# A selective scan on one core: input of state 0 made on GpSimd, end states copied on GpSimd, state sums evicted by a strand of their own, operation costs of the planner revised

## The chip, the cores and the metric

The kernel runs on one core of a Trainium2 chip. The metric is device time in microseconds (us). A run of the kernel before takes 10310.45 us, the median of three (10307.8 to 10314.3).

The engines are named as in the profile: PE is TensorE's matmul queue and PEld its weight loads, DVE is VectorE, ACT is ScalarE, POOL is GpSimd, and SP is SyncE, which here only issues DMAs. Other than SP's, no DMA queue carries the transfers of the kernel's loops.

## The reference

Four layers follow each other on an input of 8 samples x 256 channels x 32 x 32: an attention block with a convolutional feed-forward, a second attention with an MLP, a quantised bottleneck, and a Mamba layer (the fourth). The change lies in the Mamba layer, and in the cost table that orders the other three too. The Mamba layer, cut to what matters:

```python
def step(h, inp):
    u_t, dt_t, B_t, C_t = inp
    dA = jnp.exp(dt_t[:, :, None] * A)
    h = h * dA + dt_t[:, :, None] * B_t[:, None, :] * u_t[:, :, None]
    y = jnp.einsum('bdn,bn->bd', h, C_t)
    return (h, y)

x = silu(causal_conv4(x) + conv_b)               # x, z = split(u @ W_in.T)
x_dbl = x @ W_x.T                                # 16 for dt, 16 for B, 16 for C
dt = softplus(x_dbl[..., :16] @ W_dt.T + b_dt)
y = (selective_scan(x, dt, -exp(A_log), B, C) + x * D) * silu(z)
out = y @ W_out.T
```

There are 512 inner channels d and 16 states n for each. It runs over the 1024 pixels in four directions (row-wise, column-wise, and both backwards), and the four results are added. For one state n, four arrays over (channel, pixel) matter: the decay `dA`, the scan's input `dt * u * B`, the scan's result `h`, and `h * C`, which is summed over n.

## The kernel before

**Two phases.** `phase_a` does the first three layers and writes 8-bit-valued codes to DRAM. `phase_b` does the Mamba layer. In the profile phase_b begins at about 3745 us.

**Order.** The order of all instructions is fixed when the program is built. Each job is a generator (a "strand") that yields operations or conditions. `_Order.run` picks, again and again, the operation whose planned start is earliest; ties go to the lower rank. Planned starts come from `_Op.cost`, a formula for each engine and kind of operation, from `LATENCY` between engines (0.35 us), and from records of when each 512-element piece of a tile was written or read (`_Op.blocks`). The planned times decide only the order in each engine's queue. On the chip the engines wait on semaphores, in that order. Where an engine is planned to be free at the same time for several ready operations, the rank alone decides. `phase_a` uses the same planner; where PE is planned to have a gap, its `fill` puts in small bf16 matmuls.

**Blocks and groups.** A *block* n is one half (512 pixels) of one direction of one sample: 8 samples x 4 directions x 2 halves = 64 blocks. A *group* g is one state s of one block: 1024 groups. In a group the 512 channels are four tiles c of 128 partitions, worked in pairs p. `place[0]` is the group that the scans have reached.

**One group**, by strand:

- `scales` (ACT): four `dbu` tiles. The product dt*u lies transposed in `duT`, with pixels on partitions, so that B of state s is one value for each partition and ACT can multiply by it as its scale operand.
- `turns` (PE): sixteen 128x128 transposes bring `dbu` back to channels on partitions, into PSUM tiles `db` (three banks).
- `decays` (ACT): four `da` tiles, exp(dt * A), with five buffers.
- `scans` (DVE): four scans over 512 pixels, from `da` in SBUF and `db` in PSUM, into a pair tile `h` (six pairs). In a direction's second half they start from `st`, the end states of the first half.
- `ends` (ACT, only in the first half of a direction): copies the last column of each pair to `st`, two values per partition.
- `products` (POOL): each pair times the row C of state s, which `rows` (SP) loads, broadcast to 128 partitions, into `cb` (three buffers). The product is made in place. It comes only after `ends` has dealt with the pair, since `ends` reads what the product overwrites.
- `sums` (PE): transposes the product and adds it into four PSUM banks `py` over all 16 states. After the last state of three blocks in four the banks are moved to `yT`, by ACT and DVE, inside the same strand.

**Around it.** `ahead` starts the preparation of later blocks when the scans reach a given group. `mixed` makes the convolutions (`xs`) and `x_dbl` of block n+2. `steps` makes dt of block n+1, then (POOL) `tmp` = dt * xs, and its transposes into `duT`. `tables` runs silu and softplus on ACT, which takes three table loads. `outputs` makes the gate and the last product of the sample before.

The lines that the prediction's steps touch are: `_Op.__init__` (the costs), the rooms at the head of `phase_b`, `xdbl` in `mixed`, `dt` in `steps`, and the strands `scales`, `turns`, `rows`, `scans`, `ends`, `products`, `sums` and `ahead`. All instructions that the planner emits carry the one line L136 in the profile, so groups are told apart by their tiles.

Of the kernel before, what the change touches and what calls it, by code (L numbers as in the profile page):

```python
# [20 lines left out]
F32 = mybir.dt.float32  # L21
U8 = mybir.dt.uint8
BF16 = mybir.dt.bfloat16
# [6 lines left out]
P = 128  # L30
# [11 lines left out]
DC = DI // P  # L42
TH = HALF // P
PAD = 3
RND = 12582912.0
# [54 lines left out]
class _Op:  # L100


    def __init__(self, engine, method, args, kw):
        self.engine, self.method, self.args, self.kw = engine, method, args, kw
        out, ins = args[0], [a for a in (*args[1:], *kw.values()) if isinstance(a, bass.AP)]
        self.reads = {k for a in ins for k in self.blocks(a)}
        self.writes = {k for a in (out, kw.get("accum_out")) if a is not None for k in self.blocks(a)}
        self.landing = 0.0
        n = max(math.prod(a.shape[1:]) for a in (out, *ins)) / 1024
        near = all(a.space == out.space and out.space != PSUM for a in ins)  # L110
        if engine == "tensor":
            x = kw.get("rhs", ins[0])
            n = math.prod(x.shape[1:]) / 1024
            move = method == "transpose" or kw.get("is_transpose", False)
            self.cost = max(0.06, (0.22 if x.shape[0] < 20 else 0) + n * (0.93 if move else 0.44 if x.dtype != F32 else 1.76 if n > 0.2 else 2.1))
        elif engine == "vector":
            fast = near and method in ("tensor_scalar", "tensor_copy")
            both = near and method == "tensor_tensor"
            scan = method == "tensor_tensor_scan"
            self.cost = 0.04 + n * (2.2 if scan else 0.57 if fast else 1.1) + (0.3 if fast or both else 0)  # L120
        elif engine == "scalar":
            self.cost = 0.05 + 0.87 * n + (0.13 if len(ins) > 1 else 0)
        elif engine == "gpsimd":
            self.cost = 0.17 + 2.17 * n if method == "tensor_tensor" else 0.3 + n
        else:
            self.cost, self.landing = 0.1, 3.0

    @staticmethod
    def blocks(a):
        step = max(1, a.ap[0][0])  # L130
        lo = a.offset % step
        hi = lo + sum((n - 1) * abs(s) for s, n in list(a.ap)[1:])
        return [(a.name, k) for k in range(lo // 512, hi // 512 + 1)]

# [38 lines left out]
class _Order:  # L173
# [62 lines left out]
    def run(self):  # L236
        while self.strands:
# [16 lines left out]
            for o in ops:  # L254
                o.emit(self.nc)
                for k in o.reads:
                    self.read.setdefault(k[0], {})[k] = (t + cost, e)
                for k in o.writes:
                    self.written.setdefault(k[0], {})[k] = (t + cost + o.landing, e)
# [882 lines left out]
def phase_b(ctx, tc, i, col, ident, codes, w_parts, out):  # L1142
# [14 lines left out]
    xi_room = _Room(rooms, "xi", DC, [P, N + 2 * PAD])  # L1157
    xs_room = _Room(rooms, "xs", 11, [P, HALF])
    dt_room = _Room(rooms, "dt", 2 * DC, [P, HALF])
    du_room = _Room(rooms, "du", 2, [P, TH, DI])  # L1160
    db_room = _Room(rooms, "dbu", 12, [P, DI])
    da_room = _Room(rooms, "da", 5, [P, HALF])
    h_room = _Room(rooms, "h", 6, [P, 2, HALF])
    cb_room = _Room(rooms, "cb", 3, [P, HALF])
    tmp_room = _Room(rooms, "tmp", 2, [P, HALF])
    z_room = _Room(rooms, "z", DC, [P, HALF])
# [40 lines left out]
    def hs(h):  # L1207
        return slice(h * HALF, (h + 1) * HALF)
# [58 lines left out]
    def mixed(n):  # L1267
# [24 lines left out]
        def xdbl():  # L1292
# [6 lines left out]
            if d.c_d is None:  # L1299
                d.c_d = dr.tile([DS, N], F32, name="c_d", tag="c_d")  # L1300
                d.bT = sp.tile([P, NT, DS], F32, name="bT", tag="bT")
            yield S.dma_start(d.c_d[:, hs(h)], xd[DS : 2 * DS])
            done.add("xd")
# [11 lines left out]
    def steps(n):  # L1315
# [6 lines left out]
        def dt(c):  # L1322
# [11 lines left out]
            raw[n][c] = o  # L1334
            yield lambda: "soft" in done
            d.dt[c, h] = o
            t = yield from take(tmp_room)
            yield G.tensor_tensor(t, o, d.xs[c, h], ALU.mult)
            yield lambda: h in d.duT
            room, pt = yield from lend()  # L1340
            yield [T.transpose(pt[:, k * P : (k + 1) * P], t[:, k * P : (k + 1) * P], ident) for k in range(TH)]
            put(tmp_room, t)
            yield V.tensor_copy(d.duT[h][:, :, c * P : (c + 1) * P], pt.rearrange("p (t k) -> p t k", t=TH))
            put(room, pt)
            done.add(("du", c))

        return [dt(c) for c in range(DC)]


    dirs = [_Dir(b, bool(swap), back) for b in range(B) for swap in range(2) for back in (False, True)]  # L1350
    blocks = [(d, h) for d in dirs for h in d.halves]
    xis = {(b, swap): {} for b in range(B) for swap in (False, True)}
    raw = {n: {} for n in range(len(blocks))}
    gates = {(b, h): {} for b in range(B) for h in range(2)}

# [91 lines left out]


    groups = [(n, d, h, s) for n, (d, h) in enumerate(blocks) for s in range(DS)]
    dbu, db, da, hh, cbs = {}, {}, {}, {}, {}  # L1450
    place = [0]

    def scales():

        for g, (n, d, h, s) in enumerate(groups):
            yield lambda: {("du", c) for c in range(DC)} | {"bT"} <= d.done[h]
            for t in range(TH):
                src, b = d.duT[h][:, t], d.bT[:, h * TH + t, s : s + 1]
                o = yield from take(db_room)
                yield A.activation(o, src, AF.Identity, scale=b)  # L1460
                dbu[g, t] = o

    def turns():
        for g, (n, d, h, s) in enumerate(groups):
            for c in range(DC):
                yield lambda: all((g, t) in dbu for t in range(TH))
# [26 lines left out]
    def rows():  # L1493
        for g, (n, d, h, s) in enumerate(groups):
            yield lambda: "xd" in d.done[h]
            o = yield from take(cb_room)
            yield S.dma_start(o, d.c_d[s, hs(h)].partition_broadcast(P))
            cbs[g] = o

    def scans():  # L1500
        for g, (n, d, h, s) in enumerate(groups):
            step, first = -1 if d.back else 1, h == d.halves[0]
            place[0] = g
            if d.st is None:
                d.st = sp.tile([P, DC * DS], F32, name="st", tag="st")
            for c in range(DC):
                if c % 2 == 0:
# [4 lines left out]
                    x[:, ::step], da[g, c][:, ::step], db[g, c][:, ::step],  # L1512
                    0.0 if first else d.st[:, a : a + 1], ALU.mult, ALU.add,
                )
                put(da_room, da.pop((g, c)))
                put(ps_room, db.pop((g, c)))
                if c % 2:
                    hh[g, c // 2] = pair

    kept, scaled = {}, {}  # L1520

    def ends():

        for g, (n, d, h, s) in enumerate(groups):
            for p in range(2):
                yield lambda: (g, p) in hh
                pair, c = hh.pop((g, p)), 2 * p
                if h == d.halves[0]:
                    e = 0 if d.back else HALF - 1
                    o = d.st.rearrange("p (c s) -> p c s", s=DS)[:, c : c + 2, s : s + 1]  # L1530
                    yield A.copy(o, pair[:, :, e : e + 1])
                kept[g, p] = pair

    def products():
        for g, (n, d, h, s) in enumerate(groups):
            for p in range(2):
                yield lambda: (g, p) in kept and g in cbs
                pair = kept.pop((g, p))
                yield G.tensor_tensor(pair, pair, cbs[g].unsqueeze(1).to_broadcast([P, 2, HALF]), ALU.mult)
                scaled[g, p] = pair  # L1540
            put(cb_room, cbs.pop(g))

    def sums():

        for g, (n, d, h, s) in enumerate(groups):
# [27 lines left out]
            if s == DS - 1 and n % 4 != 1:  # L1573
                if n % 4 != 3:
                    yield lambda: clear[h]
                    clear[h] = False
                for t in range(TH):
                    o = yT[:, h * TH + t, :]
                    if n % 4 == 3:
                        yield V.tensor_tensor(o, py[t], o, ALU.add)  # L1580
                    elif t % 2:
                        yield V.tensor_copy(o, py[t])
                    else:
                        yield A.copy(o, py[t])
                    put(py_room, py[t])
                if g == len(groups) - 1:
                    spare.append(py_room)
                if n % 4 > 1:
                    for j in fold(d.b, d.swap, h):
                        order.add((0, n), j)  # L1590

    def ahead():

        for n in range(len(blocks)):
# [6 lines left out]
            if k is not None:  # L1601
                jobs += zip((1, 2, 3, 5, 9), mixed(k))
            if m is not None:
                jobs.append((6, tables(k, m, z)))
            if n % 4 == 1 and n + 3 < len(blocks):
# [28 lines left out]
    for rank, f in enumerate((scans, turns, products, sums, decays, scales, rows, ahead)):  # L1634
        order.add((1, rank), f())
    order.add((0, -2), ends())
    order.run()
# [118 lines left out]
```

## Time and profile before

| what | value |
|---|---|
| median of 3 runs | 10310.45 us (10307.8 to 10314.3) |
| the profiled execution, whole | 10303.42 us |
| its span, first to last instruction | 10301.6 us |
| around the span | 1.8 us |
| stretch 0 to 3600 us (phase_a): PE / DVE / ACT / POOL busy | 3386.04 / 2188.84 / 2597.26 / 897.55 us |
| first and last copy of `bT` on DVE's 63 from bank `pp` (blocks 1 to 63) | 3766.4 and 10057.7 us |
| so one block of phase_b | 6291.3 / 62 = 101.5 us |
| mean granted TensorE clock | 0.940 |

How it is read: the busy time of an engine is the union of its instructions. The records of two instructions that follow directly overlap a little on ACT and DVE: one `da` or `dbu` activation shows 710 to 714 ns, but in an unbroken row they start 0.61 to 0.62 us apart. So for loads per block the busy share is used, and for one instruction more or less the spacing. Matmul ends are modelled. Idle time is put down to the engine that the profile takes for the releaser.

### The profile page before, as it was taken

Reading aid. Unit: us, or ns where it says so; the run is one execution under the profiler, and the core shown is the slowest. Engines: PE = TensorE matmul, PEld = TensorE weight load, DVE = VectorE, ACT = ScalarE, POOL = GpSimd, SP = SyncE. Lnnn points to the kernel's source line nnn. Section 1 sums busy time; section 2 is a strip of 40 time slices with the busy share of each in tenths; the row PEclk is TensorE's granted clock in tenths of the full one; section 3 lists DMA queues with packets and bytes.
Section 4 is the critical chain, followed back from the end, with each engine's and each line's share of the span. In section 5 each row is a group of like instructions: output and inputs, shape, how many; then the busy total and the mean of one; then the engine's idle time right before and its main releaser. Section 6 shows DMA issues by size and latency. Waiting matters only on the chain.

```text
span 10301.6 us, 149772 instructions
## 1 busy us (share of the span) xinstructions
PE 9415.7 (91%) x55378; PEld 5953.1 (58%) x55499; DVE 7759.3 (75%) x8675; ACT 8514.4 (83%) x15869; POOL 6131.8 (60%) x2988
## 2 busy tenths in 40 slices
PE   9989989999999989989898999899989999989988
PEld 3333323333333347777776777777777777777676
DVE  6367467575667458888887888888888888888788
ACT  7867677867666759988898998989898889899888
POOL 1433032242121048878787787778787778787778
PEclk7988989989888899999999999999999999999999
DMA  2000000000000011112111112111111111111111
GB/s 58 30 19 17 21 21 19 17 26 17 13 17 9 17 34 51 53 44 59 46 52 53 46 52 59 43 52 56 49 51 48 56 50 49 55 52 46 57 43 52
DMA packets 219616, 415.83 MB, mean 40 GB/s; under 512 B 25137, under 2 KB 67505, under 8 KB 213762
## 3 DMA queue, kind: packets, MB, share of 16 engines
q1 hardware_dynamic: 218882, 406.24, 13.1%
q8 instruction: 437, 7.16, 0.3%
q14 instruction: 297, 2.43, 0.1%
HBM read 358.43 MB, written 37.22 MB: 38 GB/s over the span
## 4 chain that ended last, share of the span: by engine, by line
PE 28%; ACT 22%; DVE 8%; issue 3%; POOL 1%; DMA 1%; DVEq 0%; SPq 0%; POOLq 0%; ACTq 0%
PE pp L136 11%; PE py L136 9%; ACT da L136 9%; PE db L136 8%; ACT dbu L136 8%; DVE h L136 7%; ACT L136 2%; ACT xs L136 1%; ACT dt L136 1%; POOL h L136 1%; ACT L145 1%; DMA wi<-w_in 1%; DVE ys L136 1%; ACT st L136 0%; ACT z L136 0%
## 5 line engine op out<-in xcount | busy, mean ns | idle before, releaser
L136 POOL TENSOR_TENSOR h<-h,cb 128x1024 f32<-128x1024 f32 x2048 | 4813.3, 2373 | 1039.1 <-DVE h L136 367.0
L136 ACT ACTIVATE da<-dt,am 128x512 f32<-128x512 f32 x4096 | 2872.0, 714 | 543.2 <-DVE h L136 537.6
L136 ACT ACTIVATE dbu<-du,bT 128x512 f32<-128x512 f32 x4096 | 2798.1, 710 | 15.4 <-PE db L136 13.6
L136 PE MATMUL db<-ident,dbu 128*128 128x128 f32 x16384 | 2385.7, 280 | 362.2 <-DVE h L136 322.6
L136 DVE TENSOR_TENSOR_SCAN h<-da,db 128x512 f32<-128x512 f32 x2048 | 2338.9, 1202 | 460.2 <-ACT da L136 131.9
L136 DVE TENSOR_TENSOR_SCAN h<-da,st,db 128x512 f32<-128x512 f32 x2048 | 2465.9, 1262 | 258.8 <-ACT da L136 139.3
L136 PEld LDWEIGHTS db<-ident,dbu 128*128 128x128 f32 x16384 | 1885.2, 143 | 875.4 <-DVE h L136 539.6
L136 PE MATMUL py<-ident,h 128*128 128x128 f32 x16384 | 2141.8, 278 | 92.4 <-POOL h L136 75.5
L136 PEld LDWEIGHTS py<-ident,h 128*128 128x128 f32 x16384 | 1878.3, 143 | 227.0 <-POOL h L136 144.2
L136 DVE TENSOR_REDUCE stats<-bank 128x1 f32<-128x512 f32 x1536 | 983.4, 684 | 545.1 <-PE bank L136 544.0
L136 ACT ACTIVATE bank<-bank,stats 128x512 f32<-128x512 f32 x1536 | 1024.9, 672 | 432.1 <-DVE stats L136 424.5
L136 PE MATMUL bank<-big,big 32*128 32x512 f32 x4096 | 987.3, 713 | 37.9 <-ACT bank L136 27.7
L136 POOL TENSOR_TENSOR mid<-mid,mid 128x961 f32<-128x961 f32 (+2 forms) x192 | 397.2, 2076 | 992.9 <-ACT mid L136 663.6
L136 ACT ACTIVATE exps<-bank 128x512 f32<-128x512 f32 x1536 | 796.5, 620 | 165.9 <-PE bank L136 156.6
L136 PE MATMUL pp<-xi,cvd 128*128 128x512 f32 x1488 | 687.8, 598 | 1.6 <-DVE ys L136 1.6
L136 PEld LDWEIGHTS bank<-big,big 32*128 32x128 f32 x4096 | 334.7, 204 | 523.7 <-issue 219.7
L136 DVE SCALAR_TENSOR_TENSOR mid<-mid,cols,mid 128x961 f32<-128x961 f32 (+1 forms) x384 | 601.6, 1567 | 6.3
L136 PE MATMUL bank<-exps,big 128*32 128x512 f32 (+1 forms) x3072 | 547.9, 621 | 3.7 <-ACT exps L136 3.7
L136 PE MATMUL bank<-big 32*128 32x512 f32 x2048 | 517.4, 724 | 32.1 <-ACT bank L136 21.5
L136 POOL TENSOR_TENSOR tmp<-dt,xs 128x512 f32<-128x512 f32 x256 | 320.9, 1273 | 322.0 <-ACT dt L136 224.4
L136 POOL TENSOR_SCALAR big<-big,ga,gs 128x512 f32<-128x512 f32 x64 | 67.7, 1070 | 712.3 <-DVE gs L136 385.5
L136 POOL TENSOR_TENSOR big<-big,mid 128x961 f32<-128x961 f32 (+1 forms) x128 | 315.2, 2472 | 270.7 <-ACT mid L136 268.6
(204 smaller groups left out, 9116.4 us busy)
## 6 DMA issues: line engine op xcount, KB each, us to landing
cb<-c_d SPq DMA_DIRECT2D x1024, 256.0 KB, 3.3
wi<-w_in SPq DMA_DIRECT2D x192, 192.0 KB, 3.5
big<-in_x_dram SPq DMA_DIRECT2D x16, 1024.0 KB, 5.0
kept<-big SPq DMA_DIRECT2D x16, 1024.0 KB, 4.5
big<-kept SPq DMA_DIRECT2D x16, 1024.0 KB, 4.8
xf<-codes SPq DMA_DIRECT2D x48, 256.0 KB, 3.8
big<-big SPq DMA_DIRECT2D x16, 512.0 KB, 6.5
codes<-low SPq DMA_DIRECT2D x32, 256.0 KB, 2.0
```

The source lines that it names most:

```text
L136: return getattr(getattr(nc, self.engine), self.method)(*self.args, **self.kw)
L145: nc.scalar.preload_act_table_set("natural_log_exp_and_others")
```

## The change

**State 0 takes another way** (`OWN = 1`). For s = 0 `scales` and `turns` do nothing. A new strand `direct` loads the row B of state 0, broadcast to 128 partitions, and lets POOL multiply `tmp` (dt * xs, with channels on partitions) by it in place. The scans of s = 0 read this SBUF tile in place of a PSUM bank. For that, `tmp` becomes two pair tiles that are kept until these scans are done; the copy of B and C in DRAM (`c_d`) has 32 rows and not 16; and one row buffer `br` is added. `dbu` goes from 12 to 10 buffers.

**End states.** `ends` is gone. `products` copies the end states on POOL ahead of each product. `st` is four small tiles, each with two buffers.

**Eviction.** Moving `py` to `yT` becomes a strand of its own, `moved`, at rank (0, -3), the first of all.

**Times of the preparation.** The convolutions of block n+2 start at groups 0, 1, 2, 3 (1, 2, 3, 5 before), `x_dbl` at 8 (9), the tables at 4 (6). The four `tmp` products no longer follow the softplus at once: they wait for groups 5, 7, 9 and 11.

**The planner.** The costs are revised, for both phases. A DMA's read of its source lasts longer in the plan. Small tiles are tracked in pieces of 64 elements.

```diff
+OWN, AHEAD, NTMP = 1, 2, 2
+NXS, NH, NDA, NDBU = 11, 6, 5, 10
+SOFT, LATER, XD, CONV = 4, (5, 7, 9, 11), 8, (0, 1, 2, 3)
...
-            self.cost = max(0.06, ... n * (0.93 if move else 0.44 if x.dtype != F32 else 1.76 if n > 0.2 else 2.1))
+            self.cost = max(0.06, ... n * (0.96 if move else 0.44 if x.dtype != F32 else 1.76 if n > 0.2 else 2.0))
...
-            self.cost = 0.04 + n * (2.2 if scan else 0.57 if fast else 1.1) + (0.3 if fast or both else 0)
+            three = near and method == "scalar_tensor_tensor"
+            if method == "tensor_tensor_scan":
+                self.cost = 0.03 + 2.15 * n + 0.05 * points
+            elif both or three:
+                self.cost = 0.04 + 1.5 * n
...
-            self.cost = 0.05 + 0.87 * n + (0.13 if len(ins) > 1 else 0)
+            self.cost = 0.05 + 0.06 * near + 0.85 * n + 0.093 * points + 0.17 * ("accum_out" in kw)
...
-            self.cost = 0.17 + 2.17 * n if method == "tensor_tensor" else 0.3 + n
+            self.cost = 0.12 + 2.2 * n if method == "tensor_tensor" else 0.07 + (2.0 if out.dtype == BF16 else 1.5) * n
...
-                    self.read.setdefault(k[0], {})[k] = (t + cost, e)
+                    self.read.setdefault(k[0], {})[k] = (t + cost + 0.7 * o.landing, e)
...
-    db_room = _Room(rooms, "dbu", 12, [P, DI])
+    db_room = _Room(rooms, "dbu", NDBU, [P, DI])
-    tmp_room = _Room(rooms, "tmp", 2, [P, HALF])
+    tmp_room = _Room(rooms, "tmp", NTMP, [P, 2, HALF])
+    br_room = _Room(rooms, "br", 1, [P, HALF])
...
-            yield lambda: "soft" in done
+            yield lambda: "soft" in done and place[0] >= DS * (n - 1) + LATER[c]
...
+            if s < OWN:
+                continue
...
+    def direct():
+        for g, (n, d, h, s) in enumerate(groups):
+            if s >= OWN:
+                continue
+            yield lambda: "xd" in d.done[h]
+            row = yield from take(br_room)
+            yield S.dma_start(row, d.c_d[s, hs(h)].partition_broadcast(P))
+            for p in range(2):
+                yield lambda: {("du", 2 * p), ("du", 2 * p + 1)} <= d.done[h] and place[0] >= g - AHEAD
+                o = held.pop((n, p))
+                yield G.tensor_tensor(o, o, row.unsqueeze(1).to_broadcast([P, 2, HALF]), ALU.mult)
+                db[g, 2 * p] = o[:, 0]
+                db[g, 2 * p + 1] = o[:, 1]
+                used[g, p] = o
+            put(br_room, row)
...
-    def ends():
...
-                    yield A.copy(o, pair[:, :, e : e + 1])
...
-                yield lambda: (g, p) in kept and g in cbs
-                pair = kept.pop((g, p))
+                yield lambda: (g, p) in hh and g in cbs
+                pair = hh.pop((g, p))
+                if h == d.halves[0]:
+                    e = 0 if d.back else HALF - 1
+                    yield G.tensor_copy(d.st[s // 4][:, s % 4, 2 * p : 2 * p + 2].unsqueeze(2), pair[:, :, e : e + 1])
                 yield G.tensor_tensor(pair, pair, cbs[g].unsqueeze(1).to_broadcast([P, 2, HALF]), ALU.mult)
...
             if s == DS - 1 and n % 4 != 1:
...
+                order.add((0, -3), moved(n, d, h, py))
...
-                jobs += zip((1, 2, 3, 5, 9), mixed(k))
+                jobs += zip(CONV + (XD,), mixed(k))
-                jobs.append((6, tables(k, m, z)))
+                jobs.append((SOFT, tables(k, m, z)))
...
+    order.add((0, -1), direct())
-    order.add((0, -2), ends())
```

## The prediction

> **What bounds the kernel now.** I read the page's first parts, then the busy time of the stretch from block 1 to block 63, then the chain and the waits of that stretch. The stretch comes first because phase_a keeps PE busy with filler and hides phase_b in the averages.
>
> ```profile
> core 0: us, PE busy (x) PEld busy (x) DVE busy (x) ACT busy (x) POOL busy (x), PEclk, DMA share, GB/s
> 3766.00:10058.00 6292.00, 5700.34 (x38871) 4485.76 (x38986) 5319.57 (x5169) 5658.52 (x9771) 5010.39 (x2396) 0.97 0.17 51
> ```
>
> Divided by 62 blocks, a block of 101.5 us holds PE 91.9, ACT 91.3, DVE 85.8 and POOL 80.8 us. No engine is full; two are equally near, with a third close by.
>
> The chain of waits in the same stretch, shares by line (the answer itself ends in the middle of a word):
>
> ```profile
> by line: PE pp L136 17.9%; ACT da L136 13.8%; PE py L136 13.7%; PE db L136 13.2%; ACT dbu L136 11.7%; DVE h L136 10.8%; issue 4.3%; ACT L136 2.5%; ACT xs L136 2.4%; ACT dt L136 2.1%; POOL h L136 1.4%; ACT L145 1.2%; DVE ys L136 1.0%; DMA wi
> ```
>
> PE has 44.8% (pp, py, db), ACT 33.7% (da, dbu, xs, dt and the table loads), DVE 11.8%. The end is set by PE and ACT in turn, so an us taken from one of them is worth less than an us.
>
> The waits of the stretch (total us, times, longest):
>
> ```profile
> ACT da L136 <- DVE h L136: 529.3, 468, 5.2
> POOL h L136 <- ACT st L136: 336.3, 243, 8.7
> DVE h L136 <- ACT da L136: 271.2, 64, 7.4
> POOL tmp L136 <- ACT dt L136: 179.0, 31, 8.5
> DVE h L136 <- PE py L136: 162.2, 207, 4.9
> POOL h L136 <- issue: 147.1, 43, 12.5
> ```
>
> The reader is to see three things. DVE waits for `da` about once a block, 4.4 us: this is the table section on ACT (one of 7061.6 to 7072.3 us has three loads and twelve activations). POOL loses 5.4 us a block behind ACT's end copies and 2.9 us behind softplus. And the waits by `issue` are mostly POOL gaps of 12.4 us, one per 8 blocks, for which nothing in the trace stands.
>
> **What the Trainium skill says.** (1) SBUF — State Buffer, "Who interferes with whom" and "SBUF: two separate sides": a DVE instruction with two SBUF inputs contends with a GpSimd instruction that reads SBUF; the second to start waits for the first to end. Phase_b has no such DVE instruction before: each of the two-tensor kind reads one input from PSUM, and POOL's products stay within 2338 to 2489 ns. Phase_a has it, and agrees:
>
> ```profile
> L136 DVE SCALAR_TENSOR_TENSOR mid<-mid,cols,mid x384: 1199/1245/3284, 498.1 to 3297.3; 128x961 f32<-128x961 f32 x96, 128x992 f32<-128x992 f32 x96
> ```
>
> ```profile
> 516.94 8.75 DVE L136 SCALAR_TENSOR_TENSOR mid<-mid,cols,mid 128x961 f32<-128x961 f32 x3
> ```
>
> ```profile
> 516.03 11.74 POOL L136 TENSOR_TENSOR big<-big,mid 128x961 f32<-128x961 f32 x4 [3.65 <-ACT mid L136]
> ```
>
> Alone the DVE instruction takes 1.2 us (the minimum). Beside four POOL products, three take 8.75 us, 2.92 each: +1.7 us. The products take 2.94 each, against a minimum of 2.22: +0.7 us. (2) GPSIMD Engine Reference, "2.1 Instruction dispatch": each instruction costs an indirect call, tens of cycles. The nearest row here, the memset of 128x3, shows 103 ns. (3) Perfetto Trace Analysis, "GPSIMD Engine Instruction": time POOL by start-to-start spacing, not by spans. Four products in 9.41 us (from 7110.93) give 2.35 against spans of 2.37, so here both agree.
>
> **The change part by part, per block.**
>
> *Removed from ACT.* Four `dbu` at 0.615 us, the spacing of an unbroken row (7003 to 7010 us in the chain): 2.46. The end copies are 178.6 us in 62 blocks: 2.88. Together 5.34, times ACT's 33.7% of the chain: 1.80 us gained.
>
> *Removed from PE.* Sixteen transposes; the chain has eight in 0.87 us: 1.74, times 44.8%: 0.78 us gained.
>
> *Added to POOL.* Two row products at 2.37: 4.7. Sixteen copies (32 in every second block) of two values: no row shows one. Between 0.04 (eight memsets in 0.32 us) and 0.5 us, if each product waited for its copy to finish; I take 0.15, 2.4 in all. POOL goes from 80.8 to 87.9 and is covered by its 20.7 us of idle time, so nothing by itself. At 0.5 us it would be 93.5, the fullest engine, and would cost about 2 us a block.
>
> *The wait of the product for ACT's copy* goes (336.3/62 = 5.4 us). What is late next is the scan itself, which already ends most of POOL's other waits. Pairs come free sooner, which DVE sees as its 2.6 us of waiting on `py`. I count a quarter: 0.65 us gained. The early eviction acts on the same wait (PE itself waits on ACT's eviction only 10.6 us in the stretch) and is not counted again. Moved ahead of `da`, two evictions of 0.57 us on ACT could delay a scan by as much; `da` has five buffers against that.
>
> *The lock at state 0.* Four scans per block now have two SBUF inputs. A scan alone is 1.20 us, near to phase_a's instruction. Bounds: nothing if POOL happens to idle, 4 x 2.35 = 9.4 us if every scan waits for a whole product. With POOL always reading it would be 4 x 1.7 = 6.8. The four scans yield two pairs only, so POOL's backlog may run out meanwhile: I take 5 us on DVE and 2 on POOL. At that place PE has no transposes for state 0, has three banks free for state 1 and has the convolutions to do; ACT can fill five `da` and ten `dbu`. That cover takes some two thirds: 1.75 us lost.
>
> *Spread preparation and better costs.* Before, four `tmp` products stand in POOL's queue where softplus is planned, and products behind them wait (2.9 us, with 1.4 more behind PE pp). At groups 5 to 11 they come after softplus, if the tables run at group 4. What is then late is PE's transposes of `tmp`, which have until group 16. The revised costs reshuffle all queues, worth anything from +1.5 to -2 us a block: I take -0.7.
>
> *At nothing.* The row DMA: 64 of 256 KB on a queue with 1024 alike, and a DMA share of 0.17. SP waits there for the write of `c_d` (1.6 us to land), and the `cb` loads queued behind it may start 2 us late; they lead their use by two groups, some 12 us, less 3.3 to land. If that lead were gone, POOL would stall by those 2 us. The direct product waits in POOL's queue for that row and for `tmp`, with the `h` products behind it; it stands from group 14 on, the row from about 8. Two `dbu` fewer are two and a half groups of cover, where ACT now has less to do.
>
> *POOL's unexplained gaps.* If they come by number of instructions (about 309 in 8 blocks before; some 56 instead of 39 a block after), there are 3.6 more of 12.4 us. In the one at 4253.6 us, DVE loses some 5 us at its end. 18 us in all; 0 if not.
>
> *Phase_a* changes only by the costs. The DVE instruction above was planned at 1.07 us and is planned at 1.45, against a mean of 1.57; an accumulating exp is planned 0.13 longer. Real waits are nearer to the plan: -20 us, bounds -70 to +50.
>
> **Sum.** Per block -1.80 - 0.78 - 0.65 + 1.75 - 0.70 = -2.18; times 64, -140; -20 and +18 make -142. The profiled execution is 10303.4 us whole, so 10161; the median of the runs shown is 7 us above that execution: **10168 us**. Its own range is 10060 to 10285: the lock term between 0.5 and 3, the order term between its bounds in part.
>
> **The rivals.**
>
> *The lock decides.* At state 0 of each block DVE waits for whole products, POOL for scans, and POOL, at some 90 us or more, no longer catches up before the preparation comes. For it: POOL is the engine with most added, and the planner has no term for the lock. Against it: only 4 of 64 scans, with cover on PE and ACT. Without the lock the block gains 3.93; from there on the lock loses. With 6 us of up to 9.4 + 2.8 reaching the end: +2.07 x 64 - 2 = +130, **10440 us** (10335 to 10570).
>
> *ACT was the true pace.* If with 5.3 us less on ACT, and POOL free of its waits, the stalls between PE and DVE close as well, a block loses 5 us: -320 - 20, **9970 us** (9880 to 10060). For it: 8.5 us a block in which ACT waits for scans follow from the bubble of its own table section. Against it: PE remains at 90.2.
>
> *Hidden.* PE's 90.2 us set the pace and the lock eats the rest: **10310 us**, within 0.2% (20 us), which is what a measurement of this kernel can tell from no change.
>
> **Chances.** Forecast 0.57, true pace 0.13, hidden 0.08, lock 0.22. So faster 0.70, same 0.08, slower 0.22. Range 9940 to 10430: below it lie some 0.05 of the second rival, above it some 0.10 of the lock.
>
> **What would show it.** Right: about 86 us of ACT and 88 of POOL a block, no POOL wait on ACT `st`, scans without PSUM at 2 to 3 us, blocks of about 99.3 us. Wrong: such scans at 1.2 us (no lock), POOL copies far over 0.15 us, POOL above 92 us a block or heading the chain, or phase_a's end moved by over 70 us.

## The result and the profile after

The changed kernel takes 10497.4 us (median of 4 runs, 10490.4 to 10526.0), where the kernel before takes 10312.4 in the same comparison. The ratio is 1.0184, 95% interval 1.0172 to 1.0197: slower by 185 us. The forecast was 10168; what came is the rival in which the lock decides, which was put at 10440.

The span, and the busy time of each engine over the page's whole span:

```profile
span 10488.6 us, 147956 instructions
...
PE 9385.7 (89%) x54622; PEld 5897.0 (56%) x54622; DVE 8079.4 (77%) x8677; ACT 8327.6 (79%) x14587; POOL 6794.5 (65%) x4138
```

ACT and PE have less to do than before, as planned, DVE has 320 us more and POOL 663. The same stretch of phase_b as before (block 1 up to block 63), with busy us by engine, granted clock, DMA share and GB/s:

```profile
core 0: us, PE busy (x) PEld busy (x) DVE busy (x) ACT busy (x) POOL busy (x), PEclk, DMA share, GB/s
3766.00:10240.00 6474.00, 5672.90 (x37889) 4412.09 (x37888) 5575.76 (x5144) 5459.86 (x8500) 5617.54 (x3494) 0.96 0.19 52
```

The copies of `bT` run from 3746.4 to 10237.1 us, 104.7 us a block where it was 101.5. At that length a block holds POOL 90.8 us (80.8 before), DVE 90.2 (85.8), ACT 88.3 (91.3) and PE 91.7 (91.9). No engine is full now either; three that had air have lost it. Phase_a did what was forecast: the first `bT` copy, on bank `py`, moved from 3744.2 to 3722.5 us. All of the loss lies in phase_b.

The chain of waits in this stretch (the answer ends in the middle of a word):

```profile
by line: PE pp L148 16.4%; DVE h L148 14.4%; PE db L148 9.9%; PE py L148 9.7%; ACT da L148 9.6%; POOL h L148 9.2%; issue 9.2%; ACT dbu L148 8.0%; ACT L148 2.0%; ACT xs L148 2.0%; POOL tmp L148 1.8%; ACT dt L148 1.7%; DVE ys L148 1.2%; ACT L
```

POOL's products went from 1.4% to 9.2% and DVE's scans from 10.8% to 14.4%. ACT's `da` and `dbu` fell from 25.5% to 17.6%. The waits (total us, times, longest):

```profile
ACT da L148 <- DVE h L148: 865.9, 963, 7.7
...
POOL st L148 <- DVE h L148: 401.4, 258, 6.5
...
DVE h L148 <- ACT da L148: 170.7, 79, 5.9
...
POOL h L148 <- issue: 148.5, 63, 5.1
...
DVE h L148 <- PE py L148: 119.2, 144, 2.0
```

The waits that the change aimed at did shrink. POOL no longer waits for ACT's end copies, DVE's wait for `da` fell from 271 to 171 us, that for `py` from 162 to 119. What grew is the waiting for the scans, of ACT from 529 to 866 us and of POOL from 365 to 575 (585 and 414 in run x3 below, which does the same work without the lock). The scans themselves say why. Durations in ns as least/median/greatest, then first and last start:

```profile
L148 POOL TENSOR_TENSOR h<-h,cb x2048: 2327/2371/3301, 3744.3 to 10455.4; 128x1024 f32<-128x1024 f32 x187
L148 DVE TENSOR_TENSOR_SCAN h<-da,db x1920: 1182/1196/1306, 3745.3 to 10365.8; 128x512 f32<-128x512 f32 x192
...
L148 POOL COPY st<-h x1024: 175/186/1132, 3743.2 to 10380.0; 128x2 f32<-128x2 f32 x171
L148 DVE TENSOR_TENSOR_SCAN h<-da,tmp x128: 1190/1208/9265, 3738.7 to 10283.1; 128x512 f32<-128x512 f32 x128
L148 DVE TENSOR_TENSOR_SCAN h<-da,st,tmp x128: 1251/1740/3467, 3836.3 to 10374.1; 128x512 f32<-128x512 f32 x128
```

A scan from PSUM never passes 1.31 us. Those of state 0, with both inputs in SBUF, take up to 9.27. By the costliest groups they are busy 337.7 and 251.0 us, 9.20 us a block; four at the mean of PSUM scans (1.202 and 1.263) would be 4.93. DVE loses 4.3 us a block. POOL's products take 2421 ns and its copies 279 on average, where 2375 and 189 are the means without the lock (run x3 below): 1.5 + 1.4 = 2.9 us a block.

One such case, DVE's order of time:

```profile
7077.78 20.02 DVE L148 TENSOR_TENSOR_SCAN h<-da,st,db 128x512 f32<-128x512 f32 x17
7097.70 9.23 DVE L148 TENSOR_TENSOR_SCAN h<-da,tmp 128x512 f32<-128x512 f32 x1
7106.86 0.66 DVE L148 COPY dt<-pp 128x512 f32<-128x512 f32 x1
7107.44 3.44 DVE L148 TENSOR_TENSOR_SCAN h<-da,tmp 128x512 f32<-128x512 f32 x3
```

and POOL's:

```profile
7091.89 13.97 POOL L148 TENSOR_TENSOR h<-h,cb 128x1024 f32<-128x1024 f32 x6
7108.71 1.03 POOL L148 COPY st<-h 128x2 f32<-128x2 f32 x1 [2.86 <-DVE h L148]
7109.82 3.21 POOL L148 TENSOR_TENSOR h<-h,cb 128x1024 f32<-128x1024 f32 x1
```

The first scan of state 0 starts at 7097.70, in the middle of six products in a row. Products end at about 7098.9, 7101.2 and 7103.5, and the scan does not get in. It ends 1.07 us after the whole row. Then the sides change: POOL has used up its backlog, stands still for 2.9 us, and its copy and next product wait while three scans run. This is the stall that the prediction had bounded by one product, 2.35 us; here it is the whole backlog, one engine after the other.

Such a stall is the worst kind and not the usual one. Of the 256 locked scans 16 took over 9 us, each the first scan of its block, and these 16 hold nearly half of what DVE loses. Elsewhere a scan got in between two products of an unbroken row:

```profile
3938.76 11.15 POOL L148 TENSOR_TENSOR h<-h,cb 128x1024 f32<-128x1024 f32 x4
```

```profile
3942.91 1.63 DVE L148 TENSOR_TENSOR_SCAN h<-da,tmp 128x512 f32<-128x512 f32 x1
```

The second product of this row ends at 3943.46, the scan at 3944.54, and the third product shows 3.26 us. In the whole trace 44 of these scans came during a product with another directly behind it: 28 got in at the end of that product, and the 16 were passed over to the end of the row. What decides between the two is open.

The stall reaches the other engines. In the case above, from 7097.70 us, PE, PEld, DVE, ACT and POOL are busy (columns as before, the granted clock after POOL):

```profile
7097.70:7105.50 7.80, 2.40 (x20) 2.16 (x20) 7.80 (x2) 1.63 (x3) 7.80 (x4) 1.00 0.33 90
7105.50:7112.30 6.80, 4.73 (x6) 2.09 (x7) 6.49 (x6) 4.78 (x8) 3.86 (x3) 0.50 0.11 39
```

The same block in run x3, without the lock, for as long from its first scan of state 0:

```profile
6917.05:6931.65 14.60, 14.41 (x82) 9.87 (x83) 13.12 (x14) 13.10 (x22) 14.36 (x10) 1.00 0.22 70
```

PE and ACT stand idle for most of the time while the scan waits, and then the granted TensorE clock is at half for 6.8 us. The clock's records show such a stretch at half within 20 us of the start of state 0 in 63 of the 64 blocks, 339 us in all; in x3 it is one block, in x1 (state 0 as before) none. An estimate from that: up to 170 us of PE's work at full clock are lost there. Why the clock falls, the runs do not show.

### The profile page after: what moved, and what is told of

It reads as the page before. It is cut to its first block, busy times and chain, and to the rows that moved or that the text cites. A ratio compares the mean times of both kernels' runs of the same rounds, so it can differ in the third digit from the quotient of the medians.

```text
span 10488.6 us, 147956 instructions
## 1 busy us (share of the span) xinstructions
PE 9385.7 (89%) x54622; PEld 5897.0 (56%) x54622; DVE 8079.4 (77%) x8677; ACT 8327.6 (79%) x14587; POOL 6794.5 (65%) x4138
## 4 chain that ended last, share of the span: by engine, by line
PE 23%; ACT 16%; DVE 11%; POOL 8%; issue 6%; DMA 0%; DVEq 0%; POOLq 0%; SPq 0%; ACTq 0%
PE pp L148 10%; DVE h L148 9%; PE py L148 7%; PE db L148 6%; ACT da L148 6%; POOL h L148 6%; ACT dbu L148 5%; ACT L148 1%; POOL tmp L148 1%; ACT xs L148 1%; ACT dt L148 1%; DVE ys L148 1%; POOL st L148 1%; ACT L157 1%; DVE dt L148 0%
## 5 line engine op out<-in xcount | busy, mean ns | idle before, releaser
L148 POOL TENSOR_TENSOR h<-h,cb 128x1024 f32<-128x1024 f32 x2048 | 4928.8, 2421 | 439.1 <-DVE h L148 173.6
L148 ACT ACTIVATE dbu<-du,bT 128x512 f32<-128x512 f32 x3840 | 2618.8, 709 | 113.9 <-PE db L148 111.0
L148 DVE TENSOR_TENSOR_SCAN h<-da,db 128x512 f32<-128x512 f32 x1920 | 2203.1, 1202 | 369.3 <-PE db L148 158.6
L148 PE MATMUL py<-ident,h 128*128 128x128 f32 x16384 | 2177.8, 280 | 298.0 <-POOL h L148 295.0
L148 PE MATMUL db<-ident,dbu 128*128 128x128 f32 x15360 | 2240.3, 282 | 227.3 <-DVE h L148 194.5
L148 DVE TENSOR_TENSOR_SCAN h<-da,st,db 128x512 f32<-128x512 f32 x1920 | 2317.1, 1263 | 140.1 <-PE db L148 49.7
L148 PEld LDWEIGHTS db<-ident,dbu 128*128 128x128 f32 x15360 | 1792.1, 144 | 703.8 <-DVE h L148 396.0
L148 POOL TENSOR_TENSOR mid<-mid,mid 128x992 f32<-128x992 f32 (+2 forms) x192 | 398.4, 2082 | 987.7 <-ACT mid L148 670.7
L148 PE MATMUL pp<-xi,cvd 128*128 128x512 f32 x1482 | 720.7, 624 | 111.4 <-DVE dt L148 109.2
L148 POOL COPY st<-h 128x2 f32<-128x2 f32 x1024 | 286.1, 279 | 428.4 <-DVE h L148 410.6
```

The costliest lines, as they stand in the source:

```text
L148: return getattr(getattr(nc, self.engine), self.method)(*self.args, **self.kw)
```

## The experiments

All times are medians beside runs of the kernel before, whose own median moved from 10303 to 10314 us between these comparisons; a difference of that size between two rows is not read. A block is taken from the `bT` copies as above.

| run | what | us | ratio to before, 95% interval | block |
|---|---|---|---|---|
| after | the change | 10497.4 | 1.0184 [1.0172, 1.0197] | 104.7 |
| x1_own0 | state 0 as before | 10127.7 | 0.982 [0.9805, 0.9834] | 98.8 |
| x2_ends_act | end copies on ACT | 10711.3 | 1.0385 [1.0367, 1.0402] | 107.9 |
| x3_da_psum | state 0 on POOL, no lock | 10127.8 | 0.982 [0.9806, 0.9835] | 99.0 |
| x4_plan_old | old costs | 10482.1 | 1.0162 [1.0147, 1.0177] | 103.9 |
| y1b_own0_ends_act | x1, end copies on ACT | 10123.8 | 0.9821 [0.9806, 0.9835] | 99.1 |
| y2b_own0_sched_old | x1, old times | 10280.0 | 0.9969 [0.9958, 0.9979] | 101.5 |
| y3b_own0_late_evict | x1, late eviction | 10177.2 | 0.987 [0.9855, 0.9884] | 99.6 |
| y4b_half | two of four scans locked | 10327.5 | 1.0018 [1.0011, 1.0025] | 102.1 |
| z1_times_alone | before, new times | 10064.6 | 0.9761 [0.9742, 0.978] | 97.6 |
| z2_breaks | the change, more POOL copies | 10452.0 | 1.0136 [1.0121, 1.0151] | 103.9 |
| z3_psum_ends_act | x3, end copies on ACT | 10147.5 | 0.9841 [0.9826, 0.9856] | 99.2 |
| z4_own0_da8 | x1, eight `da` buffers | 10120.3 | 0.9814 [0.9799, 0.9829] | 98.7 |
| w1_later_alone | before, spread products | 10284.7 | 0.9979 [0.9969, 0.9989] | 101.1 |
| w2_earlier_alone | before, earlier convolutions, `x_dbl`, tables | 10064.8 | 0.9761 [0.9745, 0.9778] | 97.5 |
| w3_times_evict | z1, early eviction | 10092.9 | 0.9789 [0.9775, 0.9804] | 97.9 |

### Is it the lock, the load or the order?

The theory after the result (L): the scans with two SBUF inputs and GpSimd's reads shut each other out, and nothing covers it. Rivals: the new order (P), or the end copies (E).

**x1_own0**

```diff
-OWN, AHEAD, NTMP = 1, 2, 2
+OWN, AHEAD, NTMP = 0, 2, 2
```

> The changed kernel with state 0 made as before (ACT scaling and PE transposes for all 16 states; no row products, no scan with two SBUF inputs); all else of the change stays. Theory L (the lock and the row products on GpSimd cause the loss): ACT gets 2.5 us and PE 1.7 us of work per block back, but GpSimd loses 4.7 and VectorE 4.1 us, so 102 us a block or less, 10250 to 10350 us. Theory P (the new order and the new times of the preparation cause it): stays at 10450 to 10550. Theory E (the end copies on GpSimd cause it): 10400 to 10500.

10127.7 us, 370 below the changed kernel and below anything expected. Theory L's direction holds, P and E as causes of the loss fall, and the rest of the change turns out worth 185 us, not the 60 at most that L's range left it.

**x3_da_psum** keeps state 0 on POOL and takes only the second SBUF input away: ACT writes the decays of state 0 to the PSUM banks that its transposes no longer need.

```diff
 decays:
+                if s < OWN:
+                    yield lambda: n == 0 or n - 1 in turned
+                    o = yield from take(ps_room)
+                    if c == DC - 1:
+                        made.add(n)
+                else:
+                    o = yield from take(da_room)
...
 scans:
-                put(da_room, da.pop((g, c)))
+                put(da_room if s >= OWN else ps_room, da.pop((g, c)))
...
 turns:
+            if s == OWN:
+                yield lambda: n in made
...
```

> The changed kernel, but the decays of state 0 go to the three PSUM banks that the transposes of state 0 no longer use, so that its scans have one SBUF input only. The row products stay on GpSimd. If the lock is the cause (theory L in the narrow sense): scans of state 0 fall from 2.0 to 2.7 us to about 1.2 us, no GpSimd product over 2.5 us, and the time to 10200 to 10330. If GpSimd's added load is the cause and not the lock: the scans fall likewise, but the time stays at 10430 or above. The first transposes of state 1 wait longer for a bank, worth up to 1 us a block against it.

10127.8 us. The rows that answer to those above:

```profile
L148 POOL TENSOR_TENSOR h<-h,cb x2048: 2346/2373/2517, 3742.4 to 10089.7; 128x1024 f32<-128x1024 f32 x187
...
L148 POOL COPY st<-h x1024: 176/188/248, 3742.1 to 10014.8; 128x2 f32<-128x2 f32 x171
L148 DVE TENSOR_TENSOR_SCAN h<-db,tmp x128: 1186/1197/1224, 3739.7 to 9919.5; 128x512 f32<-128x512 f32 x128
L148 DVE TENSOR_TENSOR_SCAN h<-db,st,tmp x128: 1255/1259/1284, 3833.6 to 10010.5; 128x512 f32<-128x512 f32 x128
```

(`db` is here the PSUM bank that holds the decays.) The long scans, products and copies are gone, and 370 us with them (more than any range had), although POOL still makes the row products. So the second SBUF input is what costs the 370 us. The edit has one side effect: the decays of state 0 no longer take `da` buffers. In x1 three more of these are worth nothing (z4 below); with the lock present that was not tested. And since x1 and x3 take the same time, moving state 0 from ACT (2.46 us a block forecast) and PE (1.74) to POOL gains nothing on balance without the lock.

**x4_plan_old** orders the changed kernel by the old costs, pieces and read times.

```diff
...
-            elif both or three:
-                self.cost = 0.04 + 1.5 * n
...
+            self.cost = 0.04 + n * (2.2 if scan else 0.57 if fast else 1.1) + (0.3 if fast or both else 0)
...
```

> The changed kernel ordered with the cost table, the piece size and the read times of the kernel before; instructions are the same. Theory P with the costs as the culprit: 10250 to 10400 us. Theories L and E: 10450 to 10550, since the lock and the load remain.

10482.1 us: the costs are not the cause. Phase_b begins later with them (first `bT` copy at 3754.7, against 3722.5), and gains that back.

**x2_ends_act** gives the end copies back to ACT.

```diff
-                    yield G.tensor_copy(d.st[s // 4][:, s % 4, 2 * p : 2 * p + 2].unsqueeze(2), pair[:, :, e : e + 1])
...
+                    yield A.copy(d.st[s // 4][:, s % 4, 2 * p : 2 * p + 2].unsqueeze(2), pair[:, :, e : e + 1])
...
+    order.add((0, -2), ends())
```

> The changed kernel with the end copies back on ScalarE in a strand of their own, as before; state 0 still on GpSimd. Theory E: GpSimd gets 4.6 us a block back, 10300 to 10400 us. Theory L: GpSimd is relieved a little, 10430 to 10500. Theory P: 10500 or above, since ScalarE gets work back.

10711.3 us: relieving POOL costs 214 us. Theories E and L had it below 10500; P's open range (10500 or above) covers it, but P's reason, work given back to ACT, does not, since without the lock the same edit costs 20 us (z3) or nothing (y1b). Its scans of state 0:

```profile
L148 DVE TENSOR_TENSOR_SCAN h<-da,tmp x128: 1190/3010/9276, 3745.7 to 10500.0; 128x512 f32<-128x512 f32 x128
L148 DVE TENSOR_TENSOR_SCAN h<-da,st,tmp x128: 1249/3298/9273, 3842.3 to 10600.0; 128x512 f32<-128x512 f32 x128
```

Now the scans of both halves reach 9.27 us, where in the changed kernel those that follow a first half (`da,st,tmp`) stayed under 3.47. In the changed kernel copies stand between the products of the first half, so that the row that meets those scans is broken. This gave the sharper theory: a locked scan waits for a break in GpSimd's row. Counted over the trace it is too strong: here too, of the scans that came with another product directly behind, 74 got in at the next boundary and 41 were passed over.

### What lets a scan in, and what the rest is worth

**z2_breaks** tests that: a copy that nobody needs ahead of each product of the second half too.

```diff
...
+                else:
+                    yield G.tensor_copy(gap.unsqueeze(2), pair[:, :, :1])
```

> The changed kernel with more work on GpSimd: in the second half of a direction, too, a copy of two values (into a tile that nobody reads) stands ahead of each product, so that no unbroken row of products is left. If a scan with two SBUF inputs waits for a break in GpSimd's row (theory L as it stands now): the scans of 9.2 us go, and the time falls to 10350 to 10470 us though GpSimd has 2 to 4 us a block more to do. If GpSimd's load is what counts: 10500 to 10650, and the scans of 9.2 us stay.

10452.0 us: more work on POOL, 45 us less time.

```profile
L148 DVE TENSOR_TENSOR_SCAN h<-da,tmp x128: 1191/1506/3359, 3740.6 to 10228.8; 128x512 f32<-128x512 f32 x128
L148 DVE TENSOR_TENSOR_SCAN h<-da,st,tmp x128: 1250/1921/3299, 3837.9 to 10324.4; 128x512 f32<-128x512 f32 x128
```

The scans of 9 us are gone; 3.4 is a scan behind one product. With a copy next in the row the scan always got in at the end of the running product (149 of 149 here, 79 of 79 in the changed kernel). So a copy is a sure break, and the boundary of two products an unsure one. Why, these runs do not show.

**y4b_half** leaves two of the four scans locked; as x3, but for pair 0 only.

```diff
...
-                if s < OWN:
+                if s < OWN and c < 2:
                     yield lambda: n == 0 or n - 1 in turned
...
```

> As x3, but only the decays of the first pair of state 0 go to PSUM: two of the four scans keep two SBUF inputs. If each such scan pays by itself: half of the 370 us, 10280 to 10340. If the first one pays for GpSimd's whole row of products and the rest follow cheaply: 10380 to 10500, since the third scan is then the first to wait. If the row has run out by then: 10130 to 10230.

10327.5 us: 200 of 370, so each pair of locked scans pays its part.

**z3_psum_ends_act** joins x3 and x2.

> x3 (no lock, state 0 on GpSimd) with the end copies on ScalarE. GpSimd has 3 us a block less than in x3, ScalarE 3 us more. If the end copies count only as breaks for the lock: within 15 us of x3, 10110 to 10145. If GpSimd, the second fullest engine in x3, holds the time: 10050 to 10100. Beside x2 it prices the whole lock when no breaks stand in the row: 10711 less this.

10147.5 us, 2.5 us above the upper end of the range for "breaks only": without the lock the end copies on POOL are worth some 20 us with state 0 there. Beside x2 it prices the lock without breaks at 564 us. That makes three doses. DVE's time lost in locked scans, from their group's busy time as above, and POOL's in longer products and copies, against the price at the end:

| | DVE loses per block | POOL loses per block | price per block (time / 64) |
|---|---|---|---|
| y4b_half against x3 | (179.5 + 129.4) / 64 - 2.46 = 2.4 us | 1.7 us | 200 / 64 = 3.1 us |
| after against x3 | 4.3 us | 2.9 us | 370 / 64 = 5.8 us |
| x2 against z3 | (420.6 + 407.8) / 64 - 4.93 = 8.0 us | 1.4 us | 564 / 64 = 8.8 us |

At every dose the end moves by more than DVE itself loses and by less than DVE and POOL lose together. No cover of DVE's stall shows. How much of the price comes through POOL's loss and how much through the halved clock was not separated; from x3 to the changed kernel PE's busy time for the same work rises from 89.6 to 91.7 us a block.

**y1b_own0_ends_act** is x1 with the end copies on ACT (the edits of x1 and x2).

> State 0 made as before and the end copies on ScalarE as before; the rest of the change stays (costs, eviction, times of the preparation, buffers). Beside x1 it prices the end copies on GpSimd without the lock. If they are the gain of the change: 10280 to 10340 us, since ScalarE gets 2.9 us a block back and the products wait for it again. If their large price in x2 (some 214 us) came only from the lock and a full GpSimd: 10130 to 10200.

10123.8 us against 10127.7: no difference, and 6 us below the lower of the two ranges. The end copies on ACT and POOL's wait behind them are worth nothing here. They are also less work than their summed durations say: ACT is busy 91.6 us a block with them and 90.3 without, so 1.3 us and not 2.9.

**y2b_own0_sched_old** is x1 with the old times.

```diff
-SOFT, LATER, XD, CONV = 4, (5, 7, 9, 11), 8, (0, 1, 2, 3)
+SOFT, LATER, XD, CONV = 6, (0, 0, 0, 0), 9, (1, 2, 3, 5)
```

> x1 with the times of the preparation of before (tables at group 6, the four products right after softplus, convolutions at 1, 2, 3, 5, x_dbl at 9). If spreading them was worth something (I put it at 0.7 us a block with the costs): 10150 to 10250 us. If nothing: 10110 to 10145.

10280.0 us, above both ranges: the times are worth 152 us, most of the 185 that the change gains without the lock.

**y3b_own0_late_evict** puts the body of `moved` back in `sums`.

```diff
...
-                order.add((0, -3), moved(n, d, h, py))
+                if n % 4 != 3:
+                    yield lambda: clear[h]
...
```

> x1 with the eviction of the state sums inside the strand of the sums again. My prediction counted the early eviction at nothing: 10110 to 10145 us. If it frees the banks at the turn of a block in a way that counts: 10150 to 10220.

10177.2 us: the early eviction is worth 49 us in this surrounding.

**z4_own0_da8** gives x1 eight `da` buffers.

```diff
-OWN, AHEAD, NTMP = 0, 2, 2
-NXS, NH, NDA, NDBU = 11, 6, 5, 10
+OWN, AHEAD, NTMP = 0, 2, 1
+NXS, NH, NDA, NDBU = 11, 6, 8, 10
```

> x1 (state 0 as before) with eight da buffers in place of five; the room comes from the row buffer and one pair tile, which this version does not need. VectorE's wait for da behind the table section is 171 us in x1's stretch. If buffers shorten it: 9950 to 10080 us. If the section only moves the wait elsewhere: 10110 to 10145.

10120.3 us against 10127.7: the buffers are worth nothing that can be told from x1.

### One part alone, on the kernel before

**z1_times_alone** takes the new times and nothing else.

```diff
-            yield lambda: "soft" in done
+            yield lambda: "soft" in done and place[0] >= DS * (n - 1) + (5, 7, 9, 11)[c]
...
-                jobs += zip((1, 2, 3, 5, 9), mixed(k))
+                jobs += zip((0, 1, 2, 3, 8), mixed(k))
...
-                jobs.append((6, tables(k, m, z)))
+                jobs.append((4, tables(k, m, z)))
```

> The kernel before with nothing of the change but the times of the preparation: convolutions at groups 0, 1, 2, 3, x_dbl at 8, tables at 4, the four products of dt and xs at 5, 7, 9, 11. Two results stand beside it: in the changed kernel without the lock these times are worth 152 us. If they are the gain by themselves: 10130 to 10200 us. If they pay only together with the new costs and the eviction: 10230 to 10330.

10064.6 us, below the range: alone they gain 245 us, more than the change without its lock. **w1_later_alone** takes the first line of that diff, **w2_earlier_alone** the other two.

> The kernel before with one thing only: the four products of dt and xs wait for groups 5, 7, 9, 11 instead of following softplus at once; tables, convolutions and x_dbl at their old groups. z1 (these and the earlier tables, convolutions and x_dbl) gained 245 us. If the spread of the products is what pays: 10060 to 10180 us. If the earlier tables pay: 10250 to 10320.

> The kernel before with the other half: convolutions at 0, 1, 2, 3, x_dbl at 8, tables at 4, and the four products right after softplus as before. If the earlier tables pay: 10060 to 10180 us. If the spread pays: 10250 to 10330.

10284.7 and 10064.8 us. The spread of the products gives 19 us, by itself a fall of 0.2%; the earlier convolutions, `x_dbl` and tables alone take as little time as both together. The waits of w2, from 3766 us to its last block:

```profile
ACT da L136 <- DVE h L136: 301.0, 350, 4.2
...
DVE h L136 <- PE py L136: 134.9, 142, 5.9
DVE h L136 <- ACT da L136: 127.2, 54, 6.6
```

With the same work on each engine, ACT waits for scans 301 us in place of 529, and DVE for `da` 127 in place of 271. The granted clock of the stretch also rises, from 0.97 to 0.99, and PE's busy time for the same work falls from 91.9 to 90.6 us a block; how much of the gain comes that way, and which of the three start times does it, was not separated.

**w3_times_evict** adds the early eviction to z1 (the reverse of y3b's edit).

> z1 with the early eviction added, which is worth 49 us in the changed kernel without the lock. If it adds up: 10000 to 10030 us. If it pays only where the end copies or the costs of the change stand: 10050 to 10100.

10092.9 us, in the second range and worse by 28 than z1. In x1 the same edit is worth 49 us, so its sign belongs to its surroundings. w2 (and z1, level with it) is the fastest version found, ratio 0.9761.

## Why the prediction was wrong

*The lock: the step that failed is "that cover takes some two thirds: 1.75 us lost".* The place, the operation and the size were right. DVE's loss was taken as 5 us and measures 4.3, POOL's as 2 and measures 2.9, and the locked scans were forecast at 2 to 3 us and have means of 2.68 and 2.00. But 5.8 us a block reach the end. The cover was argued from what PE and ACT could do meanwhile. At all three doses at least DVE's whole loss reaches the end, and the stall at 7097.70 us shows PE busy for 2.40 of 7.80 us and ACT for 1.63, and the clock at half behind it. Nor does POOL's backlog run out early to help: in the long stalls it runs out at DVE's expense, and then POOL waits. And one product of 2.35 us was no upper bound for the wait of one scan, which can last for a whole row.

*"5.34, times ACT's 33.7% of the chain: 1.80 us gained", and PE's 0.78.* Nothing of either shows: x1 and x3 differ by state 0's share of both and agree, with the two row products on POOL set against it; y1b and x1 differ by the end copies and agree. The removal was mis-sized as well: ACT's busy time fell by 3.0 us a block (91.3 to 88.3) and not by 5.34, for the most part because the end copies were priced by their summed durations. A share of the chain says where the end was last handed on. It isn't the price of an us of that engine when three others follow at a few us.

*The product's wait for ACT (0.65 us).* The wait went, nothing came of it (y1b). The eviction, counted at nothing, gave 49 us in one surrounding and took 28 in another.

*"I take -0.7" for times and costs.* Mis-sized. The times alone are worth 152 us in x1 (2.4 a block) and 245 in the old kernel (3.8), and there it is the earlier convolutions, `x_dbl` and tables, not the spread products that the prediction argued from. The bound of -2 was too near. That the gains without the lock come to 2.5 us a block, not far from the forecast's 3.93, is luck: they come from this term and not from ACT, PE or the product's wait.

*Right:* phase_a (-22 us, forecast -20, though with the same costs it is -10 in x1 and -27 in y4b); the row DMA at nothing (its 64 loads land in 3.3 us, and x3 carries them without loss); the POOL copies (0.15 forecast; 0.19 shown without the lock, and 0.25 by start-to-start spacing: copy and product take 2.58 us in x3, a product alone 2.33). *Wrong, but small:* POOL's gaps of 12.4 us did not multiply; the longest of that kind is now 5.1, though their sum is the same (148.5 us, 147.1 before).

*The sum as measured:* all but the lock -185 us (x3), the lock +370, which makes +185. The rival with the lock had 6 us a block reaching the end, and 5.8 do; its 10440 was low because the gains that it set against them were 3.93 us a block on paper and 2.5 in phase_b in x3. It had 0.22 of the chances. The lock and its size stood in the profile before, in phase_a's rows; for the cover it held no such evidence.

## What to carry to other kernels

Where GpSimd works nearly without pause, keep each VectorE instruction to one SBUF input; in this kernel, which had PSUM banks free at that place, an operand in PSUM removed the stall at no cost that shows. Count a stall on an engine that is busy for some 85% of its block as uncovered until a run shows otherwise. And when several engines are equally near the limit, try the start times of bulky work first: two lines of start times gained 239 us here, and moving state 0 and the end copies between engines gained nothing that shows.

## What the runs showed of the hardware

- The Trainium skill's page SBUF — State Buffer ("SBUF: two separate sides") has the one who starts first hold the shared port for its whole instruction. Here a waiting scan was sometimes passed over by products that started after it: one that came during the third of six GpSimd products waited to the end of the row, past three boundaries; the longest took 9.27 us. In the changed kernel 16 of 44 scans that met such a row fared so, and 28 got in at the first boundary. With a two-value copy ahead of every product a scan waited for one product at most (3.36 us in z2).
- A locked instruction shows its wait as duration, on either side: GpSimd's copy of two values rises from 0.19 to 1.13 us, its product from 2.37 to 3.30, each by 0.94 us, a little less than one scan (1.2 us). No wait is listed for it.
- A scan with its decays in PSUM and its other input in SBUF takes the same 1.20 us as the other way round.
- The granted TensorE clock stood at half for 549 us of phase_b in the changed kernel, and for 170 us in x3, where the decays of state 0 lie in PSUM. Of the 549 us, 339 lie within 20 us of the start of state 0 (3 us in x3).
